# Where a fused attention and experts block does its rows' statistics, its modulation and its last sends

## The chip, the core and the metric

The kernel runs on one core of one Trainium2 chip. The metric is the device time of one execution in microseconds, given as the median of several runs. Beside the timed runs there is one profiled execution, whose trace gives every duration used below. It is a run of its own, with a time of its own.

## The reference

The block has an attention half and a half with a mixture of experts, both modulated by a condition `c` (adaptive layer norm). Shapes: `x` is 4 batches x 1024 tokens x 256, 16 heads of 16, 8 experts with a hidden width of 512, two experts per token.

```python
mod = (silu(c) @ wmod).reshape(4, 6, 1, 256)
sa, ca, ga, sb, cb, gb = mod[:, 0], ..., mod[:, 5]
ga = sign(ga) * max(abs(ga), 0.25)          # gb likewise
h = layernorm(x) * (1 + ca) + sa
x = x + ga * (causal_attention(h) @ W_o.T + b_o)
h = layernorm(x) * (1 + cb) + sb
logits = h @ gate_w                          # 8 experts
top2, their softmax -> combine
x = x + gb * sum_e combine_e * (silu(h @ w1[e]) @ w2[e])
```

Softmax is exact: the largest score of each row is found before the exponentials.

## The kernel before

**Units and steps.** Heads go by fours ("quads"), so there are 4 batches x 4 quads = 16 units `u = (b, qd)`. Each unit has nine steps. A step `both(u, i, u + 1, i)` does on TensorE the scores of unit `u` (L911, transposed, causal pieces) and, in turn with them, the scores of unit `u + 1` from which only row maxima are wanted (`m_parts`, L844). VectorE takes those maxima (`maxima`: `tensor_reduce` at L864, `tensor_tensor_reduce` with the causal mask at L866). ACT does the exponentials of the scores (`weigh`, L936). `finish` does the product with the values (`av_step`, L955) for the step before. PSUM has seven banks for scores and all other products, and one for the sum of `av_step`.

`max_rows(u, half)` turns the maxima of half a unit into rows: a transpose on TensorE (L876), a copy on ACT (L878), a DMA on SP's queue (L879) into spare rows of `qTs`, so that the score products come out with their maximum subtracted. The last unit has no successor and runs as `four_heads(15, i)`.

At the end of each half of a unit (twice, in steps 3 and, after the last step, 8) the accumulated `av` is copied by ACT into `ot` (L963). SP moves the sums (L970) and four heads (L973) out of it. `invert` (two or more steps later) takes the sums' reciprocals on VectorE (L976) and sends them by two DMAs (L978, L980) to a tile `rec`; `divide` multiplies `oc` by it on POOL (L987).

**Order.** Each engine works its instructions in the order that it was given. A scheduler makes that order from the program; an instruction wrapped in `in_order(...)` stays in program order on its engine, while one that is not may be moved ahead when its inputs are there. The other work of the block is cut into pieces, kept in queues, and popped a few at a time after each step: `gates`, `soon` (the `invert` and `divide` that `finish` put off), `todo` (the next batch's norm, projections, output projection), `stats`, `choices` (routing), `sends` (tokens to their experts' slots).

**Statistics.** `layer_norm_pieces` returns nine pieces per batch: eight of `bn_stats` (L44) and `bn_aggr` (L45), one per 128 tokens, and `inverse`, with a Sqrt on ACT (L50) and a reciprocal and a Newton step on VectorE (L49, L51 to L57). They are used twice: for the first norm (tiles with the ending "a", of which batches 0 and 1 are run in `ln_pieces.begin`, and batches 2 and 3 popped from `stats` one per step while `u > 0`), and for the second norm in `route_pieces` (ending "b"), where they are the first of the `choices`.

**The start.** Modulation is computed first: one third of it as columns for the first norm (`modulate`), the rest in `modulate_rest` (matmuls at L705, copies at L706, six VectorE operations on gates, and a DMA to `mods` at L714). Then the first unit's maxima are done by `m_alone(0, 0..6)`, with projections in between, then two steps of `both(0, i, 0, 7 + i)` and two of `m_alone(1, i)`.

**Routing and the handover.** After `wo_pieces(b)` has added the attention to `x`, `route_pieces(b)` chooses two experts per token, numbers the slots, and `send` (an indirect DMA of POOL, L351, for 128 tokens and one choice; ACT casts the slot numbers at L350) writes the rows into `slots` in HBM. Batches 0 to 2 are sent during attention, batch 3 in the experts' half. The first two blocks of experts' work are begun inside the last unit (`first_pieces`): loads of rows (`fetch_rows`, L515) and of two weight matrices (L523, L524), then `prepare`, which turns the rows (L545) and makes gates for them (L530 to L537). They come last in the queue `sends`, four empty pieces ahead of the two `prepare`. After the last unit come the output projection of batch 3 (L1018), the first blocks' products (L558, L569), and then the loop over the other blocks.

The lines that set how fast sends go, per step:

```python
for _ in range(2 if u + 1 == NU or u == NU - 4 and i % 2 else 1):
    if sends and sending:
        sends.popleft()()
```

Of the kernel before, what the change touches and what calls it, by code (L numbers as in the profile page):

```python
# [30 lines left out]
EPS = 1e-5  # L31
# [4 lines left out]
def layer_norm_pieces(nc, pool, x_b, eps, tag):  # L36

    nt = x_b.shape[1]
    mv = pool.tile([P, nt, 2], F32, tag=f"mv{tag}", name=f"mv{tag}")
    rs = pool.tile([P, nt], F32, tag=f"rs{tag}", name=f"rs{tag}")  # L40

    def stats(t):
        st = pool.tile([P, 6], F32, tag=f"st{tag}", name=f"st{tag}")
        nc.vector.bn_stats(st, x_b[:, t, :])  # L44
        nc.vector.bn_aggr(mv[:, t, :], st)  # L45

    def inverse():
        ve = pool.tile([P, nt], F32, tag=f"ve{tag}", name=f"ve{tag}")
        nc.vector.tensor_scalar(ve, mv[:, :, 1], EPS, None, ALU.add)  # L49
        nc.scalar.activation(rs, mv[:, :, 1], AF.Sqrt, bias=eps)  # L50
        nc.vector.reciprocal(rs, rs)  # L51

        nw = pool.tile([P, nt], F32, tag=f"nw{tag}", name=f"nw{tag}")
        nc.vector.tensor_tensor(nw, rs, rs, ALU.mult)
        nc.vector.tensor_tensor(nw, nw, ve, ALU.mult)
        nc.vector.tensor_scalar(nw, nw, -0.5, 1.5, ALU.mult, ALU.add)
        nc.vector.tensor_tensor(rs, rs, nw, ALU.mult)  # L57

    return (mv, rs), [lambda t=t: stats(t) for t in range(nt)] + [inverse]
# [21 lines left out]
def adaln_block_kernel(  # L81
# [140 lines left out]
    def route_pieces(b, misc):  # L222
# [3 lines left out]
        def begin():  # L226
            route["md"] = tmp("md", [P, 2, D])
            for k in range(2):
                nc.sync.dma_start(out=route["md"][:, k, :], in_=mods[b, 2 + k, :].partition_broadcast(P))
            route["ln"], route["ln_pieces"] = layer_norm_pieces(nc, rp, xs[b], eps, "b")  # L230
# [354 lines left out]
    with ExitStack() as actx:  # L585
# [110 lines left out]
        def modulate_rest():  # L696
# [5 lines left out]
            for n in range(2):  # L702
                ps = bank("ps_g")[0:B]
                for dc in range(NDC):
                    nc.tensor.matmul(ps, sc[:, dc, :], wm[n + 1][dc], start=(dc == 0), stop=(dc == NDC - 1))  # L705
                in_order(nc.vector.tensor_copy(rest[:, 2 * n : 2 * n + 2, :], ps.rearrange("b (i d) -> b i d", d=D)))  # L706
            g = rest[:, 0:4:3, :]
            nc.vector.tensor_scalar(sg, g, 0.0, 2.0, ALU.is_ge, ALU.mult)
            nc.vector.scalar_tensor_tensor(g, g, -1.0, g, ALU.mult, ALU.max)
            nc.vector.tensor_scalar(g, g, 0.25, None, ALU.max)  # L710
            nc.vector.scalar_tensor_tensor(rows[:, 0:2, :], sg, -1.0, g, ALU.add, ALU.mult)
            nc.vector.tensor_scalar(rows[:, 2, :], rest[:, 2, :], 1.0, None, ALU.add)
            nc.vector.tensor_copy(rows[:, 3, :], rest[:, 1, :])
            nc.sync.dma_start(out=mods, in_=rows)  # L714
# [15 lines left out]
        def ln_pieces(b):  # L730
            def begin():
                if b < 2:
                    st["ln", b], pieces = layer_norm_pieces(nc, small, xs[b], eps, "a")
# [138 lines left out]
        def max_rows(u, half):  # L872

            def run():
# [3 lines left out]
                nc.scalar.copy(rows, ps)  # L878
# [60 lines left out]
        def av_step(u, i, pts):  # L939
# [45 lines left out]
            def divide():  # L985
                rec = st.pop(("rec", u, qb))
                nc.gpsimd.tensor_tensor(  # L987
# [97 lines left out]
        for b in range(2, B):  # L1085
            st["ln", b], pieces = layer_norm_pieces(nc, small, xs[b], eps, "a")
# [10 lines left out]
        def four_heads(u, i):  # L1097
# [3 lines left out]
            pts = weigh(i, pss, True)  # L1101
            if pending is not None:
# [33 lines left out]
        modulate_rest()  # L1136
        fill = deque(keys1[4:] + [spread(1)] + v_pieces(0))
        for i in range(7):
            m_alone(0, i)
            for _ in range((2, 2, 2, 1, 2, 2, 2)[i]):  # L1140
                fill.popleft()()
            if i == 3:
                max_rows(0, 0)()
        blank_rows()
# [12 lines left out]
        for u in range(NU):  # L1157
# [22 lines left out]
            for i in range(BEGUN if u == 0 else 0, len(s_steps)):  # L1180
# [37 lines left out]
                for _ in range(2 if u + 1 == NU or u == NU - 4 and i % 2 else 1):  # L1218
# [5 lines left out]
            if u + 1 < NU:  # L1224
# [162 lines left out]
```

## Time and profile before

| | |
|---|---|
| median of 3 runs | 1053.91 us (1052.97 to 1054.21) |
| the profiled execution | 1048.28 us |
| its span (first to last instruction) | 1046.6 us |
| TensorE busy | 991.6 us (95%) |
| VectorE busy | 750.5 us (72%) |
| ACT busy | 510.2 us (49%) |
| POOL busy | 241.6 us (23%) |
| granted TensorE clock, mean | 0.98 |

By stretches of the span, TensorE was busy 24.15 of 30 us from 30 to 60, 517.33 of 523 from 182 to 705, 32.66 of 45 from 705 to 750, 54.93 of 60 from 765 to 825, and 208.29 of 221.6 after that. Engine shares are averages over such stretches, so each stage is read for itself. A timeline line gives start, duration, engine, source line, operation, out<-in, shape and count; the bracket gives how long the engine had idled before it and what released it. "PEld" is TensorE's weight load, "SPq" the sequencer of SP that issues DMAs.

### The profile page before, as it was taken

The numbers are of one execution on the slowest core, as the hardware profiler recorded it, in microseconds if no ns is written. First come the engines' busy times: TensorE is split into PE (matmuls) and PEld (weight loads), VectorE is DVE, ScalarE is ACT, GpSimd is POOL, SyncE is SP. The second block draws the span as 40 slices with busy tenths as digits, with TensorE's granted clock in tenths as the row PEclk, the third lists the DMA queues.
The fourth block names the chain that finished last, engine by engine and source line by source line (L and its number), as shares of the span: only waits on it lengthen the run. The fifth ranks groups of instructions, "written<-read, shape, count | busy, mean of one in ns | idle before, by whom it ended". The sixth has DMA issues, their size and how long they took to land. (4 is left out here: it accounts for less than half of the span.)

```text
span 1046.6 us, 22478 instructions
## 1 busy us (share of the span) xinstructions
PE 991.6 (95%) x8162; PEld 582.9 (56%) x8162; DVE 750.5 (72%) x2349; ACT 510.2 (49%) x971; POOL 241.6 (23%) x232
## 2 busy tenths in 40 slices
PE   5899999999999999999999999998689999999996
PEld 4554534534544445444454443423468878888885
DVE  5787767767787878788878788872566675656673
ACT  4225655556555565655555646536323154445440
POOL 4000010000000001312001230015143664444444
PEclk9899999999999999999999999989899999999999
DMA  8310120110111202122011231002489856443332
GB/s 280 80 32 7 39 47 14 34 39 18 38 48 50 57 23 48 50 69 82 18 43 33 73 89 35 23 27 74 157 247 348 271 118 142 76 65 67 69 60 25
DMA packets 68686, 81.58 MB, mean 78 GB/s; under 512 B 19480, under 2 KB 50072, under 8 KB 68448
## 3 DMA queue, kind: packets, MB, share of 16 engines
q1 hardware_dynamic: 55008, 63.26, 21.6%
q0 software_dynamic: 13296, 16.89, 9.1%
q8 instruction: 64, 1.05, 0.4%
q14 instruction: 46, 0.38, 0.1%
q10 hardware_dynamic: 272, 0.00, 0.0%
HBM read 45.11 MB, written 24.93 MB: 67 GB/s over the span
## 5 line engine op out<-in xcount | busy, mean ns | idle before, releaser
L936 ACT ACTIVATE pt<-ps_s 128x512 f32<-128x512 f32 x576 | 312.1, 596 | 283.2 <-PE ps_s L928 175.9
L844 PE MATMUL ps_max<-kT,qT 32*128 32x512 f32 (+3 forms) x1536 | 373.6, 526 | 7.1 <-DVE mf L864 4.1
L911 PE MATMUL ps_s<-qT,kT 32*128 32x512 f32 (+3 forms) x1536 | 341.7, 525 | 3.6 <-DMA qT<-rows 2.9
L911 PEld LDWEIGHTS ps_s<-qT,kT 32*128 32x128 f32 x1536 | 133.8, 184 | 141.2 <-issue 45.6
L864 DVE TENSOR_REDUCE mf<-ps_max 128x1 f32<-128x512 f32 x256 | 164.1, 683 | 59.8 <-PE ps_max L844 57.6
L844 PEld LDWEIGHTS ps_max<-kT,qT 32*128 32x128 f32 x1536 | 152.6, 185 | 36.9 <-DVE mx L866 12.7
L866 DVE CUSTOM_DVE_ANT_0 unused<-ps_max,cmask,mf 128x256 f32<-128x256 f32 (+3 forms) x256 | 140.6, 549 | 38.9 <-PE ps_max L844 18.9
L955 PE MATMUL av<-pt,vaug 128*32 128x512 f32 (+3 forms) x1536 | 156.9, 499 | 0.8 <-ACT ot L963 0.8
L987 POOL TENSOR_TENSOR oc<-oc,rec 64x512 f32<-64x512 f32 x32 | 40.6, 1269 | 492.8 <-DMA rec<-inv 455.6
L866 DVE CUSTOM_DVE_ANT_0 unused<-ps_max,cmask 128x128 f32<-128x128 f32 (+2 forms) x232 | 114.4, 493 | 32.9 <-PE ps_max L844 18.4
L575 POOL DMA_INDIRECT out_dram<-y,xb x67 | 108.0, 1612 | 122.8 <-DVE gs L537 38.2
L558 PE MATMUL ps_h<-xt,wa 128*128 128x256 f32 (+1 forms) x608 | 125.1, 358 | 2.2 <-DVE xt L546 2.2
L569 PE MATMUL ps_y<-wb,hs 128*128 128x256 f32 x536 | 124.1, 383 | 3.1 <-ACT hs L562 3.1
L569 PEld LDWEIGHTS ps_y<-wb,hs 128*128 128x128 f32 x536 | 101.9, 192 | 17.3 <-ACT hs L562 3.5
L558 PEld LDWEIGHTS ps_h<-xt,wa 128*128 128x128 f32 x608 | 103.7, 192 | 13.6 <-DVE xt L546 2.4
L537 DVE SCALAR_TENSOR_TENSOR gs<-x,share,gs 128x256 f32<-128x256 f32 x201 | 84.7, 478 | 1.0
L574 DVE TENSOR_TENSOR y<-ps_y,gs 128x256 f32<-128x256 f32 x67 | 25.9, 420 | 77.9 <-PE ps_y L569 74.7
L351 POOL DMA_INDIRECT slots<-hr,sloti x64 | 62.8, 982 | 75.7 <-ACT sloti L350 56.0
L955 PEld LDWEIGHTS av<-pt,vaug 128*32 128x32 f32 x1536 | 37.3, 111 | 75.8 <-issue 65.2
L562 ACT ACTIVATE hs<-ps_h 128x512 f32<-128x512 f32 x67 | 39.7, 597 | 81.5 <-PE ps_h L558 81.5
L928 PEld LDWEIGHTS <-qmask 128*32 128x32 bf16 (+1 forms) x1328 | 29.8, 97 | 64.8 <-issue 57.3
L928 PE MATMUL ps_s<-unit,qmask 128*32 128x128 bf16 (+1 forms) x1328 | 56.7, 224 | 0.0
(227 smaller groups left out, 902.2 us busy)
## 6 DMA issues: line engine op xcount, KB each, us to landing
w_s<-in_w_dram SPq DMA_DIRECT2D x16, 512.0 KB
xb<-slots SPq DMA_DIRECT2D x29, 259.0 KB
qT<-qc SPq DMA_DIRECT2D x64, 64.0 KB
kT<-kc SPq DMA_DIRECT2D x64, 64.0 KB
oc<-ot SPq DMA_DIRECT2D x128, 32.0 KB
rec<-inv SPq DMA_DIRECT2D x32, 128.0 KB
out_dram<-x SPq DMA_DIRECT2D x8, 512.0 KB
wa<-in_w_dram SPq DMA_DIRECT2D x8, 512.0 KB
```

Of the source, the lines that this page charges most:

```text
L351: sent = nc.gpsimd.indirect_dma_start(out=slots, out_offset=bass.IndirectOffsetOnAxis(ap=at, axis=0), in_=hr[:, t, :], in_offset=None,).ins
L537: nc.vector.scalar_tensor_tensor(gs[:, j, :], gb[:, b, :], share[:, j, b : b + 1], gs[:, j, :], ALU.mult, ALU.add)
L558: nc.tensor.matmul(ps[:, k, :], w[:, dc, fc * P : (fc + 1) * P], xt[:, dc, :], start=(dc == 0), stop=(dc == NDC - 1),)
L569: nc.tensor.matmul(ps[:, j, :], hs[:, fc, j * P : (j + 1) * P], w[:, fc, :], start=(fc == 0), stop=(fc == NFC - 1),)
L575: added = nc.gpsimd.indirect_dma_start(out=out_rows, out_offset=bass.IndirectOffsetOnAxis(ap=xb[:, j, D : D + 1].bitcast(I32), axis=0), in ...
L844: nc.tensor.matmul(ps[:, at : at + n], qTs[u % 3][r : r + HW, qt * P : (qt + 1) * P], kTs[u % 3][r : r + HW, kb * 512 : kb * 512 + n], sta ...
L864: nc.vector.tensor_reduce(top, ps[:, at : at + n], AX.X, ALU.max)
L866: nc.vector.tensor_tensor_reduce(out=unused[:, 0:n], in0=ps[:, at : at + n], in1=cmask[:, 512 - n : 512], scale=1.0, scalar=st["mf", u][:, ...
L911: nc.tensor.matmul(ps[:, at : at + n], kTs[u % 3][r : r + HW, kt * P : (kt + 1) * P], qTs[u % 3][r : r + HW, (qb + 1) * 512 - n : (qb + 1) ...
L928: nc.tensor.matmul(ps[k : k + w, at : at + P], qmask[:, k : k + w], unit, start=False, stop=at == masked[-1],)
L936: nc.scalar.activation(pt[:, 0:n], ps[:, 0:n], AF.Exp)
L955: nc.tensor.matmul(av[HW * j : HW * (j + 1), 512 - n : 512], vaug[b % 2][:, kt, 4 * qd + j, :], pts[j][:, at : at + n], start=(kt == 0), s ...
```

## The change

1. `layer_norm_pieces` takes `in_order` and wraps `bn_stats` and the first operation of `inverse` in it, for all its uses.
2. The statistics of batch 1 leave `ln_pieces.begin`. Two of their pieces follow each of the first four `m_alone(0, i)`, and the inverse follows the seventh.
3. `modulate_rest` returns three pieces instead of running: `columns(0)`, `columns(1)` and `gates_of_all`, put after `m_alone(0, 4)`, `(0, 5)` and `(0, 6)`. The first operation on the gates is wrapped too.
4. `max_rows(15, 1)` is run in `four_heads(15, 0)`, ahead of the pending `finish`, and its copy is on VectorE.
5. `divide` is on VectorE for the last unit and for the second half of unit 14.
6. Two sends per step in unit 14 as well as in unit 15.

```diff
-def layer_norm_pieces(nc, pool, x_b, eps, tag):
+def layer_norm_pieces(nc, in_order, pool, x_b, eps, tag):
...
-        nc.vector.bn_stats(st, x_b[:, t, :])
+        in_order(nc.vector.bn_stats(st, x_b[:, t, :]))
         nc.vector.bn_aggr(mv[:, t, :], st)
...
-        nc.vector.tensor_scalar(ve, mv[:, :, 1], EPS, None, ALU.add)
+        in_order(nc.vector.tensor_scalar(ve, mv[:, :, 1], EPS, None, ALU.add))
         nc.scalar.activation(rs, mv[:, :, 1], AF.Sqrt, bias=eps)
         nc.vector.reciprocal(rs, rs)
...
-            for n in range(2):
+            def columns(n):
                 ps = bank("ps_g")[0:B]
                 for dc in range(NDC):
                     nc.tensor.matmul(ps, sc[:, dc, :], wm[n + 1][dc], start=(dc == 0), stop=(dc == NDC - 1))
                 in_order(nc.vector.tensor_copy(rest[:, 2 * n : 2 * n + 2, :], ps.rearrange("b (i d) -> b i d", d=D)))
...
+            def gates_of_all():
+                g = rest[:, 0:4:3, :]
+                in_order(nc.vector.tensor_scalar(sg, g, 0.0, 2.0, ALU.is_ge, ALU.mult))
...
+                nc.sync.dma_start(out=mods, in_=rows)
+
+            return [lambda: columns(0), lambda: columns(1), gates_of_all]
...
-                if b < 2:
+                if b == 0:
...
-                nc.scalar.copy(rows, ps)
+                if (u, half) == (NU - 1, 1):
+                    nc.vector.tensor_copy(rows, ps)
+                else:
+                    nc.scalar.copy(rows, ps)
...
-                nc.gpsimd.tensor_tensor(
+
+                eng = nc.vector if u + 1 == NU or (u + 2 == NU and qb == 1) else nc.gpsimd
+                eng.tensor_tensor(
                     oc[at : at + 64, cols], oc[at : at + 64, cols], rec[at : at + 64, :], ALU.mult
                 )
...
             pts = weigh(i, pss, True)
+            if i == 0:
+                max_rows(u, 1)()
             if pending is not None:
                 finish(pending)
...
-        modulate_rest()
+        others = modulate_rest()
+        st["ln", 1], lines = layer_norm_pieces(nc, in_order, small, xs[1], eps, "a")
...
             for _ in range((2, 2, 2, 1, 2, 2, 2)[i]):
                 fill.popleft()()
+
+            for f in (lines[2 * i : 2 * i + 2] if i < 4 else others[i - 4 : i - 3]):
+                f()
             if i == 3:
                 max_rows(0, 0)()
+        lines[-1]()
...
-                for _ in range(2 if u + 1 == NU or u == NU - 4 and i % 2 else 1):
+                for _ in range(2 if u + 2 >= NU or u == NU - 4 and i % 2 else 1):
...
-            if u + 1 < NU:
+            if u + 2 < NU:
                 todo.appendleft(max_rows(u + 1, 1))
```

More of the change, by code (lines that the diff above doesn't have):

```diff
@@ L229, in begin @@
                 nc.sync.dma_start(out=route["md"][:, k, :], in_=mods[b, 2 + k, :].partition_broadcast(P))
-            route["ln"], route["ln_pieces"] = layer_norm_pieces(nc, rp, xs[b], eps, "b")
+            route["ln"], route["ln_pieces"] = layer_norm_pieces(nc, in_order, rp, xs[b], eps, "b")
         def ln(*ks):
@@ L706, in modulate_rest @@
                 in_order(nc.vector.tensor_copy(rest[:, 2 * n : 2 * n + 2, :], ps.rearrange("b (i d) -> b i d", d=D)))
[L707 to L714, printed above, removed]
+            def gates_of_all():
+                g = rest[:, 0:4:3, :]
+                in_order(nc.vector.tensor_scalar(sg, g, 0.0, 2.0, ALU.is_ge, ALU.mult))
+                nc.vector.scalar_tensor_tensor(g, g, -1.0, g, ALU.mult, ALU.max)
+                nc.vector.tensor_scalar(g, g, 0.25, None, ALU.max)
+                nc.vector.scalar_tensor_tensor(rows[:, 0:2, :], sg, -1.0, g, ALU.add, ALU.mult)
+                nc.vector.tensor_scalar(rows[:, 2, :], rest[:, 2, :], 1.0, None, ALU.add)
+                nc.vector.tensor_copy(rows[:, 3, :], rest[:, 1, :])
+                nc.sync.dma_start(out=mods, in_=rows)
+            return [lambda: columns(0), lambda: columns(1), gates_of_all]
         def blank_rows():
@@ L731, in begin @@
             def begin():
-                if b < 2:
-                    st["ln", b], pieces = layer_norm_pieces(nc, small, xs[b], eps, "a")
+                if b == 0:
+                    st["ln", b], pieces = layer_norm_pieces(nc, in_order, small, xs[b], eps, "a")
                     for f in pieces:
@@ L1085, in adaln_block_kernel @@
         for b in range(2, B):
-            st["ln", b], pieces = layer_norm_pieces(nc, small, xs[b], eps, "a")
+            st["ln", b], pieces = layer_norm_pieces(nc, in_order, small, xs[b], eps, "a")
             stats.extend(pieces)
```

## The prediction, made before the changed kernel was run

> **What bounds the kernel now.** I read the page's slices first (one is 26.2 us, a digit its busy tenths), and the two largest groups of instructions (busy time and mean ns, idle time before them and its releaser):
>
> ```profile
> PE   5899999999999999999999999998689999999996
> PEld 4554534534544445444454443423468878888885
> DVE  5787767767787878788878788872566675656673
> ...
> L936 ACT ACTIVATE pt<-ps_s 128x512 f32<-128x512 f32 x576 | 312.1, 596 | 283.2 <-PE ps_s L928 175.9
> L844 PE MATMUL ps_max<-kT,qT 32*128 32x512 f32 (+3 forms) x1536 | 373.6, 526 | 7.1 <-DVE mf L864 4.1
> ```
>
> TensorE is full nearly everywhere (991.6 of 1046.6 us). It has holes in two places: the first two slices, and those around 710 to 765, where attention hands over to the experts' blocks. The two groups add that in between TensorE waits for VectorE next to nowhere (7.1 us before 1536 matmuls of maxima, 4.1 of it one wait in the start), while ACT waits for TensorE. So VectorE work taken from or put into units 1 to 14 is worth little, and only the two holes can give much.
>
> The timeline of the start on TensorE (start, duration, what, in brackets the idle time before and its releaser):
>
> ```profile
> 30.77 3.60 PE L705 MATMUL ps_g<-wm,sc 128*4 128x512 f32 x8
> 34.29 1.36 PE L844 MATMUL ps_max<-kT,qT 32*128 32x512 f32 x8
> ...
> 42.49 3.26 PE L844 MATMUL ps_max<-kT,qT 32*128 32x384 f32 x14 [4.08 <-DVE mf L864]
> ```
>
> and VectorE's line that released it:
>
> ```profile
> 41.75 2.48 DVE L864 TENSOR_REDUCE mf<-ps_max 128x1 f32<-128x512 f32 x4
> ```
>
> Maxima lie ready at 35.65, but VectorE reduces the first at 41.75: it is still at statistics of later batches, which the scheduler has put first.
>
> The handover, TensorE's timeline:
>
> ```profile
> 720.14 0.71 PE L911 MATMUL ps_s<-qT,kT 32*128 32x256 f32 x8 [2.43 <-DMA qT<-rows]
> ...
> 743.63 1.09 PE L545 MATMUL ps_mi<-ident,kc 128*128 128x128 f32 x4 [5.43 <-DMA kc<-slots]
> 748.37 1.09 PE L545 MATMUL ps_mi<-ident,kc 128*128 128x128 f32 x4 [3.65 <-DMA kc<-slots]
> ...
> 751.25 3.82 PE L1018 MATMUL ps_mi<-wg,oc 128*128 128x256 f32 x16
> ```
>
> POOL's, where the sends stop:
>
> ```profile
> 736.84 1.28 POOL L987 TENSOR_TENSOR oc<-oc,rec 64x512 f32<-64x512 f32 x1 [3.52 <-ACT pt L936]
> 738.40 1.01 POOL L351 DMA_INDIRECT slots<-hr,sloti  x1 [0.28 <-POOL oc L987]
> ```
>
> and SP's, which fetches the two blocks' rows:
>
> ```profile
> 740.90 0.36 SPq L515 DMA_DIRECT2D kc<-slots  x1
> ...
> 743.29 0.34 SPq L515 DMA_DIRECT2D kc<-slots  x1
> ```
>
> The last send to the slots waits on POOL behind a division, which itself waited 3.52; 2.5 us after it the first block's rows are fetched, and TensorE stands 5.43 and 3.65 for the two blocks. Attention's own work was over at 738.2 but for the last AV.
>
> **Part 1: the handover (row maxima of (15,1), sends by two, divisions).**
> - Row maxima of (15,1): the transpose L876 ran at 713.46, ACT's copy at 715.00, but the DMA L879 stood on SP behind L970 and four L973 (715.18 to 718.25) and went at 718.36. Now transpose and copy come ahead of AV(14,8), so L879 goes ahead of those five at about 713.1: the wait of 2.43 goes, and attention ends at 735.8. The five DMAs behind it start where they did, their data being the later.
> - Sends by two in unit 14 too: of 15 real sends, before, four went in steps 5 to 8 of unit 14 and eleven in unit 15. Now eight and seven; the last goes in step (15,3), and no division stands before it, since those go to VectorE. ACT casts its slot numbers behind the copy of ot (726.95 before, 2.4 earlier now, 0.6 long), so it is sent at about 725.3 and landed 2.5 later (738.40 to 740.90 before) at 727.8. SP is then at the fourth oc DMA (to about 728.0), so the first fetch goes at 728.3, 12.6 earlier than 740.90.
> - What is late next: both blocks' prepares now stand in step (15,6), ahead of the scores of step 7. TensorE is there at 735.8 - 5.3 (four pieces of scores and AV at 1.0 to 1.5) = 730.5. Rows of block 0 come 2.6 after issue (740.90 to 743.51): 731. The second fetch goes 2.4 behind the first, past two weight loads, and takes 5.0 (743.29 to 748.25): 735.7, and 1.09 of transposes: TensorE resumes at 736.8. Then 5.3 for the rest and 1.5 for the last AV: L1018 at 743.6 in place of 751.25, -7.6. Of the 12.6 of the fetch, 5 are lost to TensorE standing still in the middle of attention.
> - Queues: inverse and reciprocal rows of (15, half 0) (L978, L980) are now behind the two fetches and four weight loads on SP (about 4 us). Only division (15,0) waits for them, and its consumer L1018 is at 743.6; covered.
> - Divisions on VectorE: POOL's take 1.25 to 1.28. No row shows VectorE at 64x512 with two SBUF inputs; the nearest, L709 on 512 elements, took 0.67. Only the last one is on the path (L1018's second half, at 767.16, waited 1.30 for it): -0.6. The Trainium skill ("SBUF — State Buffer", Who interferes with whom) has a rule against it: a VectorE instruction with two SBUF inputs and a GpSimd one that reads SBUF exclude each other. Three such at 0.67 beside POOL's sends would cost at most 2.0, if sends were late; with the fetch 5 us ahead of the second block's rows I take 0.
>
> Weights after 765 follow by chains of loads (DMA share 0.99 in 765 to 825), so they shift along. Sum of part 1: -7.6 - 0.6 = -8.2, with ends -3 (rival b) and -11 (the second block's rows as fast as the first's 2.6).
>
> **Part 2: statistics of batches 2 and 3.** Sixteen bn_stats at 0.39 with aggregate at 0.17, overlapping, make 8.8; they leave VectorE's first 42 us and go, with two inverses, one piece per step into units 1 and 2. These had 26.75 VectorE busy of 37.4 and 30.2 of 41.0. With 5 us more each they stand at about 85%. Bounds 0 and 8.8. Units 2 and 6 (30.2 and 35.4 busy, 41.0 and 43.0 long, between the DMAs of their second rows of maxima) differ by 0.38 per us of VectorE work, and most of that is unit 6's own additional TensorE work; I take 0.14 of 10 us, 0.7 a unit: 1.4.
>
> Each inverse also puts a Sqrt between exponentials; before, batch 2's and 3's ran in the start. One of the four such detours that the trace shows, for a route's statistics:
>
> ```profile
> 314.26 1.28 ACT L50 ACT_TABLE_LOAD   x1
> 316.21 0.30 ACT L50 ACTIVATE rsb<-mvb,eps 128x8 f32<-128x8 f32 x1 [0.66 <-DVE mvb L45]
> 316.53 1.28 ACT L936 ACT_TABLE_LOAD   x1
> ```
>
> ACT gives 2.86 (1.28 + 0.30 + 1.28). The Trainium skill ("ScalarE: Activation LUTs", What ACT_TABLE_LOAD costs) speaks against this more strongly: a drain of 1.38 besides each load, so 5.3 for two switches. The row shows next to none: load, 0.30, load follow without a gap but for the wait on mvb, and exponentials go on at 317.82. By the row two detours are 5.7, by the rule 10.6; were all of it exposed, my sum below would be +0.1 by the row and +5.0 by the rule. I go by the row. ACT is half empty (half of each step), and over the four TensorE's waits on that result were 2.0, 1.7 and 1.5 in all, those of the handover among them; I take 0.5 each: 1.0.
>
> **Part 3: route statistics.** Pinned, those of batches 0 and 1 leave their place right after the additions (units 5 and 9) and come two to a step in the first four steps of units 6 and 10: 1.14 of VectorE per step where about 0.85 of 4.8 is free. 0.3 x 4 over, twice, less half for the relieved units: +1.2 (bounds 0 and 4.6).
>
> **Part 4: the start.** From 35.3 on VectorE loses 6.12 (35.30 to 41.75) and batch 1's second normalising piece (1.38 at 86.35, later now), and takes on batch 1's statistics between sets of maxima (4.4), its inverse (0.9), the two modulation copies (1.3), the gates (2.6) and batch 1's first normalising piece (1.38, at 30.71 before): 10.6. Free before: 4.8 of 41.75 to 67, and 2.5 of 67 to 88. VectorE begins its maxima about 6.1 earlier, so 10.6 in is met by 7.5 out and by what was free. TensorE's four modulation matmuls (3.60 in two halves of 1.8) leave 30.77, where they filled the wait for keys (DMA to 34.29), and are bare now: +3.6 against the 4.08 saved. SP: the modulation rows' DMA L714 moves behind spread(2). Net 0 (-5 to +3).
>
> **Sum:** -8.2 + 1.4 + 1.0 + 1.2 + 0 = -4.6. The profiled execution took 1048.28 (span 1046.6 and 1.7 around it): about 1043.7. It lies 5.6 below the median of the runs shown, so on the median 1053.91 - 4.6 = 1049.3.
>
> **Rivals.**
> - (a) Slower: work moved into VectorE and ACT of units 1, 2, 6 and 10 is exposed. It amounts to 8.8 + 5.7 + 4.6 = 19. From about 45% exposed on it eats the 8.2. For: VectorE stands at 85% there and waits for the Sqrt's result with its reciprocal queued before maxima, and scores then lack banks. Against: ACT's and TensorE's wait columns. At 60%: 11.4 - 8.2 = +3.2, 1057; all: 1065.
> - (b) No change: the second block's rows land later than 735.7, as its weights (0.5 MB each) share the DMA engines with the rows, and TensorE stands in mid-attention. A gain of 3 is left, 1053.5. For: before, 5.0 against 2.6. Against: nothing else is on the queues then.
> - (c) Faster still: VectorE's earlier start in the prologue passes through (4.08 kept, the matmuls of modulation beside other waits): -4 more, 1045.
> - The scheduler can still float what is not pinned (aggregate, reciprocal, gates after the first). By the built order the statistics do stand where the change puts them, so I give this nothing of its own.
>
> **How the numbers follow.** Forecast 0.45 (1047 to 1051.5), (c) 0.17, (b) 0.2, (a) 0.18. A measurement of this kernel tells about 0.2% (2.1 us) from no change: faster 0.45 + 0.17 = 0.62, same 0.20, slower 0.18. The range takes in (c) and (b) and (a)'s first half: 1044 to 1056.5.
>
> **What would show it.** Right: no wait on qT<-rows in the last unit; the first kc<-slots near 728; TensorE waiting at L545 for about 5 once, mostly for the second block; L1018's first near 744 less the shift so far; first maxima reduced near 36. Wrong: units 1 and 2 longer by over 2 each, waits of L911 on ACT after L50 of 1 or more, or VectorE's maxima as TensorE's releaser in units 6 and 10; a fetch still after 735.

## The result, and the profile after

The changed kernel took 1068.57 us (median of 4 runs, 1066.79 to 1071.31) beside 1053.44 for the kernel before, run next to it (4 runs, 1048.28 to 1054.21): a ratio of 1.0152, with a 95% interval of [1.0114, 1.0190]. Run again later as e12, it had a ratio of 1.0097 [1.0064, 1.0129]. It is slower, by 1.0 to 1.5%, where the prediction had it faster by 4.6 us (range 1044 to 1056.5). A ratio is worked out over all undisturbed runs, so it differs a little from the quotient of the two medians.

The granted TensorE clock before, by slices:

```profile
PEclk9899999999999999999999999989899999999999
```

The page after, its span, slices and the two groups of before:

```profile
span 1065.0 us, 22467 instructions
PE   5899999999999999999999999998889989999995
PEclk9879999999999999999999999999899999999998
...
L944 ACT ACTIVATE pt<-ps_s 128x512 f32<-128x512 f32 x576 | 313.5, 596 | 302.1 <-PE ps_s L936 189.5
L849 PE MATMUL ps_max<-kT,qT 32*128 32x512 f32 (+3 forms) x1536 | 379.7, 529 | 7.2 <-DVE mx L871 4.5
```

TensorE is busy for 1011.5 us in place of 991.6, and idle for 53.5 in place of 55.0: the 18.4 us of span are no new idle time, the matmuls take longer. The waits before the maxima's matmuls are the same too (7.2 in place of 7.1), and their busy time is 379.7 in place of 373.6. One row that says why is PEclk, the granted clock. It dips in the second and third slice, and the mean fell from 0.980 to 0.973. Four projection matmuls that took 1.03 us at full clock take 2.07 at half (below). Added up over windows of 1 us (length times missing share of the clock), half clock took at most 28.2 us after and 21.0 before, so up to 7.2 of the 18.4; the rest is in matmuls that count as busy while something else sets their pace, which the page can't split. The profiled execution of before was the fastest of its four runs, so 18.4 is more than the medians differ by (15.1).

To place the loss I follow one event through both traces: the start of each DMA that brings rows of maxima into `qTs` on SP's queue (two per unit; L879 before, L887 after; the first is the first unit's).

| event | before | after | difference |
|---|---|---|---|
| unit 0's first rows | 57.05 | 54.26 | -2.8 |
| unit 0's second rows | 76.34 | 85.08 | +8.7 |
| fourth DMA (the start is over) | 119.53 | 127.51 | +8.0 |
| ninth (units 1 and 2 are over) | 214.10 | 226.38 | +12.3 |
| 14th and 15th (half of unit 6 lies between) | 322.57, 338.92 | 333.78, 354.86 | +11.2, +15.9 |
| last but one (unit 15's first rows) | 688.42 | 707.28 | +18.9 |
| first matmul of the last output projection (L1018, L1028) | 751.25 | 768.53 | +17.3 |

Start +8.0, units 1 and 2 +4.3, routes up to the handover +6.6, handover -1.6, the rest +1.1: together 18.4. The prediction had 0, +2.4, +1.2 and -8.2.

Single profiles differ by chance too. Five of the kernels below (e1, e3, e5, e6, e11) are the same as before up to the ninth DMA; against before's profile they stand at -0.2 to +1.3 us at the fourth and at -0.5 to +1.1 at the ninth. Differences of profiles below are good to about 1 us, not better.

**The start.** TensorE's timeline after, for the lines of before at 30.77 to 42.49:

```profile
30.26 1.03 PE L793 MATMUL ps_mi<-hT,wk_s 128*128 128x256 f32 x4
33.45 3.55 PE L849 MATMUL ps_max<-kT,qT 32*128 32x512 f32 x8 [2.17 <-DMA kT<-kc]
36.93 2.07 PE L793 MATMUL ps_mi<-hT,wq_s 128*128 128x256 f32 x4
...
53.56 0.38 PE L881 MATMUL ps_mi<-ident,mx 128*16 128x128 f32 x1 [2.69 <-DVE mx L869]
...
72.98 1.83 PE L849 MATMUL ps_max<-kT,qT 32*128 32x512 f32 x2 [1.25 <-DVE mx L871]
```

and VectorE's first maxima, for the line at 41.75:

```profile
34.58 1.89 DVE L869 TENSOR_REDUCE mf<-ps_max 128x1 f32<-128x512 f32 x3 [15.95 <-PE ps_max L849]
```

VectorE does begin 7.2 us earlier, as predicted (about 36), and has stood idle for 15.95 before it. But where the modulation's matmuls were, TensorE now stands for 2.17 until the first keys land. The same eight matmuls of maxima take 3.55 in place of 1.36, for the most part still at full clock: they go in four pairs that start at 33.45, 34.03, 34.64 and 35.33, about as far apart as the four DMAs of keys were issued (0.61), where before the pairs ran together, the keys having landed during the modulation. From 35.7 on it has half clock, and the four projections take 2.07 in place of 1.03. The view by windows of 2 us (stretch, length, then busy time and count of TensorE, its weight loads, VectorE, ACT and POOL, then granted clock, DMA share, GB/s) shows it:

```profile
34.00:36.00 2.00, 2.00 (x8) 0.88 (x6) 1.42 (x3) 0.00 (x0) 0.00 (x0) 0.93 0.42 80
36.00:38.00 2.00, 2.00 (x5) 0.89 (x4) 1.43 (x3) 0.00 (x0) 0.00 (x0) 0.50 0.55 98
38.00:40.00 2.00, 2.00 (x6) 1.63 (x5) 0.74 (x4) 0.47 (x1) 0.00 (x0) 0.50 0.39 68
40.00:42.00 2.00, 2.00 (x10) 0.87 (x12) 0.00 (x0) 0.47 (x1) 0.00 (x0) 0.50 0.40 74
42.00:44.00 2.00, 2.00 (x24) 1.63 (x17) 0.88 (x4) 0.00 (x0) 0.00 (x0) 0.86 0.00 0
```

Half clock from about 35.7 to 42.5, 6.8 us, in which TensorE is full and yet loses up to 3.4. The waits of 2.69 and 1.25 stand beside two more such stretches (52.8 to 59.6 and 73.3 to 80.1). Before, the start had one, at 41.5 to 48.4, beside its wait of 4.08. The windows of the whole start, from 26 us to the fourth DMA of rows, before and then after:

```profile
26.00:119.53 93.53, 87.38 (x685) 46.64 (x687) 75.38 (x232) 36.25 (x73) 1.94 (x3) 0.96 0.20 43
```

```profile
26.00:127.51 101.51, 94.58 (x683) 47.91 (x685) 70.84 (x203) 36.45 (x71) 1.94 (x3) 0.90 0.19 41
```

Of the +8.0, TensorE's idle time is 0.8 (6.9 in place of 6.2) and half clock up to 6.8 (20.5 us long in place of 6.8).

**The handover.** TensorE's timeline after, for the lines of before at 720.14 to 751.25:

```profile
738.91 0.40 PE L963 MATMUL av<-pt,vaug 128*32 128x256 f32 x1 [0.61 <-issue]
...
745.48 2.07 PE L919 MATMUL ps_s<-qT,kT 32*128 32x512 f32 x2 [2.22 <-ACT pt L944]
...
755.46 0.66 PE L545 MATMUL ps_mi<-ident,kc 128*128 128x128 f32 x4
759.33 1.12 PE L545 MATMUL ps_mi<-ident,kc 128*128 128x128 f32 x4 [3.22 <-DMA kc<-slots]
```

ACT's, POOL's and SP's:

```profile
744.83 2.06 ACT L944 ACTIVATE pt<-ps_s 128x512 f32<-128x512 f32 x4 [5.05 <-remote]
...
747.73 0.96 POOL L351 DMA_INDIRECT slots<-hr,sloti  x1 [4.80 <-ACT sloti L350]
...
751.56 0.36 SPq L515 DMA_DIRECT2D kc<-slots  x1
```

The wait of 2.43 on `qT<-rows` is gone, and no division stands right before the last send any more, as predicted. Yet the last send waits 4.80 for its slot numbers, because ACT itself stood for 5.05 with a releaser that the profile calls "remote", while TensorE's matmuls came singly with "issue" before them.

### The profile page after: what moved, and what is told of

Its sections match the earlier page's. It is cut to its first block, busy times and chain, and to the rows that moved or that the text cites. A ratio compares the mean times of both kernels' runs of the same rounds, so it can differ in the third digit from the quotient of the medians.

```text
span 1065.0 us, 22467 instructions
## 1 busy us (share of the span) xinstructions
PE 1011.5 (95%) x8162; PEld 589.1 (55%) x8162; DVE 757.7 (71%) x2353; ACT 518.2 (49%) x974; POOL 234.9 (22%) x229
## 5 line engine op out<-in xcount | busy, mean ns | idle before, releaser
L849 PE MATMUL ps_max<-kT,qT 32*128 32x512 f32 (+3 forms) x1536 | 379.7, 529 | 7.2 <-DVE mx L871 4.5
L919 PE MATMUL ps_s<-qT,kT 32*128 32x512 f32 (+3 forms) x1536 | 352.9, 530 | 4.2 <-ACT pt L944 2.2
L919 PEld LDWEIGHTS ps_s<-qT,kT 32*128 32x128 f32 x1536 | 136.1, 185 | 146.7 <-issue 52.0
L997 POOL TENSOR_TENSOR oc<-oc,rec 64x512 f32<-64x512 f32 x29 | 37.1, 1279 | 443.5 <-DMA rec<-inv 395.7
L351 POOL DMA_INDIRECT slots<-hr,sloti x64 | 63.0, 985 | 74.3 <-ACT sloti L350 53.8
```

Source lines behind the costliest of these rows:

```text
L351: sent = nc.gpsimd.indirect_dma_start(out=slots, out_offset=bass.IndirectOffsetOnAxis(ap=at, axis=0), in_=hr[:, t, :], in_offset=None,).ins
L849: nc.tensor.matmul(ps[:, at : at + n], qTs[u % 3][r : r + HW, qt * P : (qt + 1) * P], kTs[u % 3][r : r + HW, kb * 512 : kb * 512 + n], sta ...
L919: nc.tensor.matmul(ps[:, at : at + n], kTs[u % 3][r : r + HW, kt * P : (kt + 1) * P], qTs[u % 3][r : r + HW, (qb + 1) * 512 - n : (qb + 1) ...
```

## The experiments

Ratios are to the kernel before, run next to them: its median was 1053.78 beside e1 to e4, 1052.35 beside e5 to e8, 1054.58 beside e9 to e12 and 1055.66 beside e13 and e14. A single profile's end says less than these ratios: the 43 runs of the kernel before beside e13 and e14 went from 1048.2 to 1064.7, and over the 59 beside e1 to e4 the time rose by about 7.8 us for each 0.01 of mean granted clock that was missing.

### The handover: whole, and in parts

e1: before, with the handover's part of the change alone (points 4 to 6 of the change).

> The kernel before with the three edits at the end alone: rows of maxima of (15,1) early, divisions of the last halves on VectorE, sends by two in unit 14; statistics and modulation as before. The prediction's sum for these was -8.2 us (1053.4 to about 1045). The profile of the changed kernel shows TensorE and ACT slowed while seven sends follow each other on POOL (ACT idle 5.05 us, TensorE waiting for its own sequencer), and the last send 8 us late. Theory A, that sends by two cause this: the gain of 2.4 from the row maxima and 0.6 from the division is lost again, 1051 to 1056, with the same idle stretch of ACT in the trace. Theory B, that it was an accident of that execution or of the later start: 1044 to 1048, and the first rows of a block fetched near 728.

Measured 1052.81, ratio 0.9983 [0.9959, 1.0008]. e5 has only the rows of (15,1) early:

```diff
+                if (u, half) == (NU - 1, 1):
+                    nc.vector.tensor_copy(rows, ps)
...
+            if i == 0:
+                max_rows(u, 1)()
...
-            if u + 1 < NU:
+            if u + 2 < NU:
```

> The kernel before with the rows of maxima of (15,1) early alone (transpose ahead of the product of (14,8), copy on VectorE); divisions and sends as before. In the three profiles that have all three end edits, TensorE and ACT crawl for 6 to 9 us in steps 1 to 3 of the last unit, in gaps that no event explains. If the crawl comes from the sends, this kernel keeps its 2.4: 1050.5 to 1052.5 against 1053.8, without the crawl. If it comes from TensorE running through those steps without the pause of 2.43 that it had, the crawl is here too and the gain is lost: 1053 to 1058.

1050.82, 0.9979 [0.9954, 1.0004]. The fetch stays late (740.41). TensorE's timeline of e5:

```profile
743.19 1.08 PE L545 MATMUL ps_mi<-ident,kc 128*128 128x128 f32 x4 [8.66 <-DMA kc<-slots]
748.36 1.09 PE L545 MATMUL ps_mi<-ident,kc 128*128 128x128 f32 x4 [4.09 <-DMA kc<-slots]
751.25 4.49 PE L1021 MATMUL ps_mi<-wg,oc 128*128 128x256 f32 x16
```

The wait on rows turned whole into a longer wait on the slots: L1021 starts at 751.25, where L1018 had. e6 has only the sends by two:

```diff
-                for _ in range(2 if u + 1 == NU or u == NU - 4 and i % 2 else 1):
+                for _ in range(2 if u + 2 >= NU or u == NU - 4 and i % 2 else 1):
```

> The kernel before with the sends by two in unit 14 alone; rows of maxima and divisions as before. If the crawl of TensorE and ACT comes from the sends (five to seven in a row on POOL, first columns of the second choice, while TensorE multiplies with the values of step 1), it is here: ACT idle for 2 us and more with no releaser in steps 1 to 3, and the end no earlier, 1052 to 1057. If the sends are innocent, the block's rows are fetched about 8 earlier and TensorE waits less for them: 1046 to 1050.

1049.07, 0.9970 [0.9954, 0.9987]: here this part is a gain by itself (but see e10). e11 has rows and sends, with the divisions left on POOL.

> The kernel before with early rows of maxima and sends by two, divisions on POOL as before. Each alone gave about 2 to 3 us, all three edits only 1. If moving the divisions to VectorE is what costs: 1047 to 1049, without the crawl of TensorE and ACT in steps 1 to 3 of unit 15. If the crawl comes from early rows and early sends together (TensorE meets the run of sends while it goes through the steps with the masks): 1051 to 1054, with the crawl.

1050.99, 0.9965 [0.9942, 0.9987]. TensorE's timeline of e11:

```profile
734.66 0.66 PE L545 MATMUL ps_mi<-ident,kc 128*128 128x128 f32 x4 [0.47 <-DMA kc<-slots]
739.20 1.11 PE L545 MATMUL ps_mi<-ident,kc 128*128 128x128 f32 x4 [3.88 <-DMA kc<-slots]
...
748.40 0.92 PE L1021 MATMUL ps_mi<-wg,oc 128*128 128x256 f32 x3
```

and two windows of it:

```profile
740.00:742.00 2.00, 2.00 (x10) 0.52 (x8) 2.00 (x6) 0.00 (x0) 0.00 (x0) 0.50 0.75 250
742.00:744.00 2.00, 2.00 (x34) 0.89 (x34) 1.77 (x4) 1.32 (x3) 0.00 (x0) 0.89 0.04 3
```

This run stood 1.55 behind before at the last but one DMA of rows (689.97 against 688.42). On before's clock, its first fetch (731.78) went at 730.2, the second block was there at 737.65, L1021 began at 746.85: 4.4 of the predicted 7.6 are there. e1 and e11 do not differ beyond their intervals, so the divisions on VectorE are not shown to gain or to cost anything: TensorE's wait for the last one (1.30 before) is 0.58 in the changed kernel, but 1.35 in e1.

### Statistics of batches 2 and 3 in units 1 and 2

e2 pins these alone; the statistics of batches 0 and 1 and those of the routes float as before.

```diff
+        in_order(nc.vector.bn_stats(st, x_b[:, t, :]))
...
+        in_order(nc.vector.tensor_scalar(ve, mv[:, :, 1], EPS, None, ALU.add))
...
-            st["ln", b], pieces = layer_norm_pieces(nc, small, xs[b], eps, "a")
+            st["ln", b], pieces = layer_norm_pieces(nc, in_order, small, xs[b], eps, "a")
```

> The kernel before with the statistics of batches 2 and 3 alone pinned to their place in units 1 and 2 (batches 0 and 1, the route's and modulation as before). The prediction gave the units +2.4 (statistics 1.4, Sqrt between exponentials 1.0), with VectorE free earlier in the start (its first maxima about 3 us earlier). The trace of the changed kernel has +4.6 between the row-maxima DMAs of these two units. If the exposed share is as in that trace: 1055 to 1058, less 0 to 3 for the start. If the prediction's share was right: 1053 to 1056.

1054.50, 1.0001 [0.9969, 1.0032]. By the fourth and ninth DMAs of rows, the start gained 5.8 and units 1 and 2 gave back 6.9. By the views by windows, 4.1 of the 5.8 is idle time of TensorE, and up to 1.7 is half clock: the stretch of 6.8 beside the old wait is gone, and one of 3.4 has come at 51.6. Where, VectorE's timeline of e2 shows (L866 is the causal maxima, its accumulator read left out here):

```profile
142.87 0.20 DVE L51 RECIPROCAL rsa<-rsa 128x8 f32<-128x8 f32 x1 [0.74 <-ACT rsa L50]
142.99 0.30 DVE L866 CUSTOM_DVE_ANT_0 unused<-ps_max,cmask,mf 128x128 f32<-128x128 f32 x1
...
143.21 1.17 DVE L54 TENSOR_TENSOR nwa<-rsa 128x8 f32<-128x8 f32 x1
144.31 0.60 DVE L866 CUSTOM_DVE_ANT_0 unused<-ps_max,cmask,mf 128x384 f32<-128x384 f32 x1
```

with ACT's and POOL's:

```profile
141.24 1.28 ACT L50 ACT_TABLE_LOAD   x1
142.53 0.30 ACT L50 ACTIVATE rsa<-mva,eps 128x8 f32<-128x8 f32 x1
142.85 1.28 ACT L936 ACT_TABLE_LOAD   x1
...
143.10 1.26 POOL L987 TENSOR_TENSOR oc<-oc,rec 64x512 f32<-64x512 f32 x1 [5.97 <-DMA rec<-inv]
```

VectorE stands with the reciprocal at the head of its queue until the Sqrt is done, 0.74, with maxima behind it. Then a product of 8 numbers takes 1.17, where it took 0.17 in the start of before (29.27), and ends with POOL's division at 144.36. TensorE waits 1.07 for maxima at 144.97, and from about 147.2 to 154.0 it has half clock.

Two ways to take this away. e8 takes the Sqrt off ACT: the roots of batches 2 and 3 come from Newton steps on POOL.

```diff
+            nc.gpsimd.tensor_scalar(rs, ve, -0.5, 1.5, ALU.mult, ALU.add)
+            for _ in range(3):
+                nc.gpsimd.tensor_tensor(q, rs, rs, ALU.mult)
...
-        nc.scalar.activation(rs, mv[:, :, 1], AF.Sqrt, bias=eps)
-        nc.vector.reciprocal(rs, rs)
```

> As the run with late statistics of batches 2 and 3 alone, but their inverse roots are made by Newton steps on POOL from ve, so no Sqrt and no table load stands between the exponentials of units 1 and 2 (16 bn_stats stay there on VectorE). In the run with the Sqrt units 1 and 2 together were 6.9 longer than before, 3.4 of it at half clock in the half of unit 1 where the Sqrt is. If the Sqrt with its two loads is the larger part: 2 to 3 are left of the 6.9, and the time is 1049 to 1051. If VectorE's statistics are: 5 to 7 are left, 1053.5 to 1055.5.

1059.77, 1.0087 [1.0051, 1.0123], slower than with the Sqrt: units 1 and 2 give back 12.5. VectorE's and TensorE's timelines of e8:

```profile
150.44 0.17 DVE L63 TENSOR_TENSOR nwa<-rsa 128x8 f32<-128x8 f32 x1 [3.18 <-POOL rsa L57]
...
151.87 1.13 PE L772 MATMUL ps_mi<-wv_s,hT 128*128 128x256 f32 x4 [2.79 <-DVE mf L873]
```

POOL's 13 small operations of 0.20 take 3.6 us one after another, and VectorE stands 3.18 for them with its maxima behind; TensorE waits 2.79 here and 2.72 for the second inverse, and two stretches of half clock follow. This miss told more than a hit: the ACT detour is not what makes most of the loss, VectorE's queue holding the consumer of a round trip ahead of maxima is. e9 keeps the Sqrt and makes two pieces of `inverse`, the Sqrt in one step, the pinned reciprocal and Newton step in the next:

```diff
+    def root():
+        nc.scalar.activation(rs, mv[:, :, 1], AF.Sqrt, bias=eps)
...
+    def newton():
+        first = in_order if apart else lambda inst: None
+        first(nc.vector.reciprocal(rs, rs))
```

> As the run with late statistics of batches 2 and 3 alone, but the inverse is in two pieces: the Sqrt on ACT, and one step later (pinned) the reciprocal and the Newton step on VectorE. So VectorE never stands in its queue for the Sqrt (0.74 and 1.07 in that run), nor, in unit 1, for POOL's division (its multiplication of 0.16 took 1.17 there). The 16 bn_stats and the two Sqrt with their table loads stay in units 1 and 2. If VectorE's standing and the half clock after it make most of the 6.9 that the units lost: 2 to 4 are left of it, the start keeps its 5.7, and the time is 1048 to 1050.5 (kernel before about 1053). If the statistics themselves or ACT's detour make it: 5 to 7 are left, 1053 to 1055.

1052.42, 0.9970 [0.9946, 0.9993]. VectorE's timeline of e9:

```profile
150.59 0.19 DVE L52 RECIPROCAL rsa<-rsa 128x8 f32<-128x8 f32 x1
150.82 0.17 DVE L56 TENSOR_TENSOR nwa<-rsa 128x8 f32<-128x8 f32 x1
```

No wait, 0.17 for the product, no half clock in units 1 and 2, which now give back 3.3 of a start's gain of 5.4. The time alone does not part e9 from e2 (the intervals overlap); the traces do. What is left of the 6.9 is neither idle time nor half clock: TensorE's matmuls are busy 3.2 longer than before (97.35 in place of 94.11). With half clock taken off, this is 2.3 in e8, which has no ACT detour, and 2.4 in e2, which has it. So most of it goes with the statistics on VectorE, and the detour of 2.86 was covered but for 1 at most.

### The routes' statistics

e3 pins these alone (`in_order` for the tiles with ending "b").

> The kernel before with the route statistics alone pinned (two pieces per step in the first four steps of units 6 and 10, Sqrt behind them), all else as before. The prediction gave +1.2. In the trace of the changed kernel units 5, 6, 9 and 10 together grew by 6.6, of which 1.7 is a stretch at half clock in unit 6. If that growth belongs to the pin: 1057 to 1060, with the first half of unit 6 at about 20 instead of 16.35. If it came from elsewhere: 1053.5 to 1055.5.

1057.94, 1.0022 [0.9994, 1.0050]; by the DMAs of rows +2.5 in the first half of unit 6, +4.0 after unit 10. The windows of these halves, before and then e3:

```profile
322.57:338.92 16.35, 16.35 (x169) 8.65 (x164) 12.47 (x44) 8.20 (x16) 0.00 (x0) 1.00 0.09 22
```

```profile
321.49:340.33 18.84, 18.08 (x150) 9.00 (x152) 15.66 (x60) 10.98 (x19) 0.00 (x0) 1.00 0.08 18
```

VectorE's work rose by 3.2, the stretch by 2.5. Here only 3.9 of 16.35 had been free, in gaps between sets of maxima; in e3 VectorE stands for none of note from 319.4 to 337. The ratio's interval would still allow the +1.2 of the prediction; the traces speak against it: in the five profiles with this pin (e3, e4, e7, after, e12) this half takes 18.65 to 21.10, in the eleven without it 16.35 to 16.74.

### The modulation

e4 is the changed kernel with `modulate_rest` run whole at its old place:

```diff
-        others = modulate_rest()
+        for f in modulate_rest():
+            f()
```

> The changed kernel with the rest of modulation run in one piece at its old place (matmuls, copies, gates, DMA), batch 1's statistics still between the sets of maxima. Theory C, the clock: the matmuls of modulation had kept TensorE busy while it waited for keys; without them it idles 2.17 us and is then granted half speed for 6.8 us. With them back the stretch from 35 to 43 is at full clock, and 3.4 for it and some of the bare 3.6 of matmuls come back: 1061 to 1064, against 1068.6. Rival, that VectorE's added work is what costs: its work is the same 10 us, only earlier, so at most 1 us comes back: 1067 to 1069.

1058.07, 1.0044 [1.0020, 1.0067], against 1.0152 and 1.0097 for the change. After the start it stands at -0.4 in place of +8.0 (fourth DMA of rows), with one stretch of half clock (3.4 us long) in place of three (20.5). TensorE's timeline of e4:

```profile
32.56 3.60 PE L706 MATMUL ps_g<-wm,sc 128*4 128x512 f32 x8
36.08 1.45 PE L849 MATMUL ps_max<-kT,qT 32*128 32x512 f32 x8
```

No wait for keys, full clock. Against e2's start (-5.8) it is 5.4 behind: e4 has batch 1's statistics between the first sets of maxima, e2 has them in VectorE's idle time before. Half clock is the same in both starts; 2.2 of the 5.4 is idle time of TensorE, the rest matmuls that count as busy.

e7 is the changed kernel with those matmuls done a second time at the old place; nothing reads what they write. It adds work, only to keep TensorE busy there:

```diff
+        for n in range(2):
+            ps = bank("ps_g")[0:B]
+            for dc in range(NDC):
+                nc.tensor.matmul(ps, sc[:, dc, :], wm[n + 1][dc], start=(dc == 0), stop=(dc == NDC - 1))
```

> The changed kernel with four matmuls more, at the place that modulation's rest had (the same shapes, into a bank that nothing reads): TensorE is busy while it waits for keys, and VectorE has exactly the changed kernel's work. Theory C, the clock: no stretch at half clock from 35 to 43, the first maxima sooner, 3 us or a little more back: 1063 to 1066 (1068.6 without). Rival, VectorE's added work and the bare matmuls: nothing back, 1068 to 1070.

1059.78, 1.0072 [1.0046, 1.0099]. TensorE's timeline of e7:

```profile
31.85 3.60 PE L1152 MATMUL ps_g<-wm,sc 128*4 128x512 f32 x8
35.37 1.85 PE L849 MATMUL ps_max<-kT,qT 32*128 32x512 f32 x8
```

With 3.6 us of matmuls more, the start ends 3.7 earlier (+4.25 in place of +7.98), and the half clock at 35.7 to 42.5 is gone. 2.6 of the 3.7 are there at the first rows; the rest may be chance, since the second stretch is 3.4 long here and 6.8 in the changed kernel. The ratio's interval overlaps that of e12, so the time alone wouldn't show it; the trace does. e14 turns it round: before, with the modulation's move alone.

> The kernel before with modulation's rest alone in three pieces after sets 4, 5 and 6 (statistics and end as before, so VectorE is still busy until about 39 with later batches' statistics). In the changed kernel this move was worth 8 us of the start: about 4 of it came back with matmuls that only kept TensorE busy, 4 are bare matmuls and gates. Here TensorE waits for VectorE at about 38 anyway, so if the clock is the cause it may only change where the slow stretch falls, and the bare part of 3 to 5 is left: 1056 to 1059. If the move costs its 8 by itself, whatever VectorE does: 1060 to 1063. If VectorE's work is what counts, which is the same here in sum: 1053 to 1055.

1058.85, 1.0004 [0.9975, 1.0033], so by the time not to be told from nothing. Its profile has the wait for keys (1.85), 3.29 for the first maxima, three half-clock stretches, and +3.8 after the start, having been at -5.3 at the first rows. Alone the move also clears VectorE's queue, which in the whole change the statistics' move has done already; that it costs its full price only there is argued from this, and fits.

One more comparison shows how much chance there is in half clock. Before and e6 are the same kernel up to unit 14, and in both TensorE waits 1.77 for maxima here:

```profile
56.46 0.28 PE L876 MATMUL ps_mi<-ident,mx 128*16 128x128 f32 x1 [1.77 <-DVE mx L864]
57.00:60.00 3.00, 3.00 (x20) 1.78 (x16) 2.18 (x4) 1.31 (x2) 0.00 (x0) 1.00 0.26 46
```

```profile
56.65 0.28 PE L876 MATMUL ps_mi<-ident,mx 128*16 128x128 f32 x1 [1.77 <-DVE mx L864]
57.00:60.00 3.00, 3.00 (x11) 1.32 (x12) 1.19 (x2) 1.50 (x2) 0.00 (x0) 0.51 0.24 41
```

Before keeps full clock, e6 gets half. In each trace, the beginnings and ends of all half-clock stretches lie whole multiples of 3.413 us apart (after: 35.7, 52.8, 73.3 and 349.7 are 5, 6 and 81 of them apart). This grid lies differently in e6: its stretches begin at 43.4 and 57.0, before's at 41.5. So the same wait can fall well or badly in the grid, and one profile's half clock in the start is good to about 1.7 us.

### The change again, and a better version

e12 is the changed kernel once more.

> The changed kernel once more, unaltered, on this chip beside the others, for its spread and a second profile: 1065 to 1070, with stretches at half clock at about 35, 52 and 73 in the start. If the crawl in unit 15 is of the program and not of one execution, it is in this profile too.

1065.72, 1.0097 [1.0064, 1.0129]; half clock again at 36.7 to 43.5, 53.8 to 60.6, 74.3 to 81.1 and 350.7 to 354.1, so both executions of the changed kernel that were profiled have the same stretches. e10 takes e9's late statistics and the sends:

> The run before this one and the sends by two in unit 14 together. If the gains of the parts are at different places and add up: the gain of the split alone and 3 more (1045 to 1048). If the second half of what sends by two gave was chance: 1048 to 1051.

1052.71, 0.9983 [0.9959, 1.0008], where the two alone would add up to 0.994: on top of e9 the sends are not seen to gain. e13 adds the early rows to it, with divisions on POOL, batch 1's statistics and the modulation at their old places and the routes unpinned:

> The kernel before with the three things that gained alone: late statistics of batches 2 and 3 with the inverse in two pieces, early rows of maxima of (15,1), sends by two in unit 14 (divisions on POOL, route statistics and modulation as before). The three gave 0.3% each against the kernel before. If they add up, 1046 to 1048.5 where the kernel before is at about 1053.5; if the end gives the same 3 us however it is reached, 1049 to 1051.

1048.93, 0.9947 [0.9929, 0.9966]: faster than both kernels. Why it gains where e10 did not, no run shows. The head of its page (the profiled execution, 1042.83, was the fastest of its 22 runs):

```profile
span 1041.1 us, 22469 instructions
...
PE   5999999999999999999999999999889899999995
```

## Why the prediction was wrong, part by part

**The start: 0 predicted, +8.0 measured.** This is the largest error, and the step that failed. The prediction wrote that the modulation's matmuls "filled the wait for keys (DMA to 34.29), and are bare now: +3.6 against the 4.08 saved". The sum took the matmuls' own duration and left the granted clock out of every term. The start again, from 26 us to the fourth DMA of rows, with TensorE's idle time and the length of its half-clock stretches, of which half is lost at most:

| kernel | length | idle | at half clock | lost by it at most |
|---|---|---|---|---|
| before | 93.5 | 6.2 | 6.8 | 3.4 |
| e2 | 87.7 | 2.1 | 3.4 | 1.7 |
| e4 | 93.1 | 4.3 | 3.4 | 1.7 |
| e7 | 97.8 | 4.8 | 10.2 | 5.1 |
| after | 101.5 | 6.9 | 20.5 | 10.2 |
| e12 | 102.6 | 6.9 | 20.5 | 10.2 |

So up to 6.8 of the 8.0 is half clock. Three terms, each the difference of two profiles:
- VectorE freed of late statistics: -5.8 (e2 against before). The prediction's 4.08 was the wait alone; 1.7 of half clock went with it.
- Batch 1's statistics between sets of maxima: +5.4 (e4 against e2), none of it half clock. Before, they lay in VectorE's idle time ahead of the first maxima, of which 15.95 is now left empty. The prediction met them with "what was free" later on.
- The modulation's move: about +8 (e4 against after), with up to 8.5 more lost to half clock. Some 3.7 of it is bought back by matmuls that only keep TensorE busy (e7), although they are 3.6 of added work. The other 4.6 (e7 against e4) come between the first and the second rows, where the moved matmuls stand (59.61 and 64.41, 1.88 each) with their copies and gates between maxima; up to 3.4 of it is half clock. At the first rows the changed kernel is only 0.5 behind e4, so the lost cover for the keys is the smaller part of the 8.

The Trainium skill ("TensorE: Matmul & The Clock Gate", What's actually happening) says that the clock falls to half after an idle window of about 3.4 us and comes back after a busy one, windows running freely. This rule spoke against the change, and the prediction did not weigh it. The stretches here are 3.4, 6.8, 10.2 or 13.7 long, which agrees with the window; but gaps well below it, of 2.17, 2.69 and 1.25, have such stretches beside them, and for these the rule taken at its word would have charged nothing: it would have warned of the kind of loss, not given its size.

**Units 1 and 2: +2.4 predicted, +4.3 measured (e2: +6.9).** ACT's detour was priced by the row at 2.86 and the row held: load, root, load without a drain, in e2 as in after. The exposed wait was put at 0.5 each, on ACT. It is on VectorE, where the reciprocal holds the queue (0.74 and 1.07, in e2 as in after), then in a product of two SBUF inputs beside POOL's division (0.17 to 1.17 in e2, to 0.85 in after), and in e2 in the clock. In after, TensorE's waits in these units come to 1.7, not far from the 1.0 that was predicted; the term that was mis-sized is the statistics' 1.4: TensorE's matmuls are busy 3.1 longer (97.21 in place of 94.11; 2.3 to 3.2 in e2, e8 and e9). Rival (a) had named "waits for the Sqrt's result with its reciprocal queued before maxima"; its sum charged nothing for the clock either. The rule of the Trainium skill ("SBUF — State Buffer", Who interferes with whom) on a VectorE instruction with two SBUF inputs, which the prediction priced at 0 for the handover, fits what happens here in units 1 and 2, where it had not been looked for: the long product ends with POOL's, at 144.4.

**Routes: +1.2 predicted, +4.0 (e3) to +6.6 (after, with all else between) measured.** The average share of VectorE's free time per step (0.85 of 4.8) was right as a mean; the work lands beside a maximum of its load. After adds a stretch of half clock at 349.7 to 353.2 to it, with only 0.11 of idle time on TensorE in the 3.4 us before.

**The handover: -8.2 predicted; -4.4 for e11's L1021, -1.6 in the changed kernel's profile.** By the ratios, e1 gained 1.8 (interval -0.8 to 4.3) and e11 3.7. The direction was right: rows early, sends earlier, TensorE standing once for the second block (3.9 to 4.5 in e1 and e11; 5 was predicted). Three sizes were off. The fetch goes 1.9 later than the 728.3 said: in e11 the last send began at 728.20 (726.65 on before's clock, 725.3 said), and from it to the fetch were 3.6 in place of 2.5. The rest of attention behind the second block takes 8.1 (740.31 to 748.40) in place of 6.8, with half clock to 742.4, which makes about 1 of the 1.3; in e1 and e6, where half clock goes on to 745.5 and 746.5, it takes 8.8 and 9.1. Last, in e1 and in after TensorE and ACT slow down before that, in gaps that no event explains: ACT [2.68] and [2.49] "remote" in e1, 5.05 in after.

**In sum.** The parts alone measured 0.9983 (handover), 1.0001 (late statistics), 1.0022 (routes) and 1.0004 (modulation). Together that is next to no change. e4, the whole change but the modulation's move, is at 1.0044; the change is at 1.0097 and 1.0152. So more than half of the loss comes with the modulation's move on top of the others. What e4 has beyond handover, late statistics and routes (1.0006 together) fits batch 1's statistics, which no run had alone. Half clock is not the whole: over e12's runs the mean granted clock was 0.9756, over the 60 runs of before beside them 0.9773, only about 2 us more lost to it. In the profiles the changed kernel has less of it elsewhere: before's stretch at 690 to 700 has no counterpart in it. The prediction's rival (a) was on the right side, for part of the right reason; the largest term, the start at half clock, stood among no rivals.

**Open.** What "remote" is. It appears with many sends in a row; it was 5.05 in the profile of the changed kernel and about 1 in e12, which is the same kernel. e6 and e7 send as much without it. That the divisions on VectorE bring it on fits e1 and e4 (2.5 to 2.7) against e6, but not e7 and e12, and e10, e11 and e13 have about 1 of it without them. What sets the pace of the matmuls in the other 12.7 us of added busy time (19.9 less 7.2), no view splits.

## What to carry to other kernels

Price a gap on TensorE by its length and by the half clock that may follow it: with "filler" matmuls in a wait of 2 us, 3.6 us of added work, the start ended 3.7 us earlier here. Before moving work out of idle time, ask what the idle time was good for; a batch of statistics that was free before the first maxima cost 5.4 us between them, by the difference of two profiles. A piece that needs another engine's result is pinned one step behind the request, never in the same piece: on an in-order queue its wait is everybody's behind it (e2 to e9, 6.9 to 3.3 us in units 1 and 2).

## What the runs showed of the hardware

- A wait of 1 to 3 us in dense work was followed by half clock at several places (1.07 in e2 at 144.97: 6.8 us; 2.17 in after at 33.45: 6.8), but not always: one of 1.77 was followed by it in e6 and not in before, where the code is the same. A stretch in after (349.7) has only 0.11 of idle time in the 3.4 us before it.
- Beginnings and ends of half-clock stretches lie on a grid of 3.413 us in every trace; where the grid lies differs from execution to execution (first stretch of the same start at 41.5 in before, at 43.4 in e6).
- One VectorE operation on 8 numbers per partition took 1.17 in place of 0.17, and ended together with POOL's 1.26 us product (in after it took 0.85): most of a POOL operation's length is what a small VectorE one may cost.
- A run of 13 POOL operations, 0.20 each, took 3.6 us, 0.28 from one to the next.
